# A graph and convolution layer on one core: the normalisation of the first batches on another engine, their turning and their rows issued as two streams, and both batch norms' constants asked for together

## The chip, the core and the metric

The kernel runs on one core of a Trainium2 chip. The metric is the device time of one execution in microseconds (us); the time before is the median of three runs, 2063.89 us (2061.74 to 2067.14). The engines are named as the profile names them: PE (TensorE, matrix products and turning), PEld (its weight loads), DVE (VectorE), ACT (ScalarE), POOL (GpSimd) and SP (SyncE, which issues most of the loads).

## The reference, cut to what matters

There are 32 batches of 512 nodes with 256 features. Each is normalised along its features and clipped at zero (h), and the layer's result is added to x:

```python
h = jnp.maximum(_layernorm(x, axis=-1), 0.0)
# inside the layer, on h:
c = relu(_bn(conv1(h), bn1))            # 1 tap
c = _bn(conv2(c), bn2)                  # 17 taps along the nodes
x_conv = relu(c + h)
s = h @ w_se.T + b_se                   # 3 values per node
A = exp(-|s_i - s_j|^2) * adj
x_nmp = A @ relu(h @ w_msg.T + b_msg)
gi, gh = [x_conv, x_nmp] @ w_ih.T + b_ih, h @ w_hh.T + b_hh
r, z = sigmoid(gi_r + gh_r), sigmoid(gi_z + gh_z)
out = x + (1 - z) * tanh(gi_n + r * gh_n) + z * h
```

The batch norm is an affine map per channel: scale = g / sqrt(v + eps), shift = b - m * scale. All data are 32-bit floats.

## The kernel before

Features lie on the partitions for all matrix work, so each batch is first normalised with its nodes on the partitions and then turned. The kernel is written as five streams (generators): *rows* (first convolution of each batch, written as rows into the tile h), *begins* (turning the batches from number 4 on), *graphs* (messages, kernel exponentials, masks, gather), *conv* (the second convolution, in a fast form of 25 products for each of seven groups of columns; the name ps_c) and *gates* (ps_acc). A planner in Python, which runs while the program is built, keeps an estimated time `now`, advanced by each TensorE instruction, and an estimated time at which DVE and ACT become free. It lets one stream issue at a time: the one that is furthest behind by its own clock among those whose condition holds. So the program is one fixed order on each engine, and each engine works its queue in that order. When no stream can issue, the planner waits in steps of 0.25 and now and then issues a transpose of the identity into an unused bank (`keep_warm`, line 143).

DVE and ACT work that no stream asks for directly comes from `fill` (line 1282): when DVE is free soon, `background` (line 1260) issues a piece of normalisation, of the second convolution's weights (`weights_first`, names g, gg, w, from the raw weights wraw) or of its operands (names x, xd).

The parts that the change and the steps of the prediction touch:

- `norm(b)` (line 349) normalises batch b in pieces. DVE makes the statistics of four chunks of 128 nodes (bn_stats, bn_aggr), adds eps (veps), POOL raises to the power -0.5 (`rsqrt`, line 275; names rstd), DVE makes the shift, and ACT applies scale and shift to each chunk, 128x256 (line 371). For batch 0 the chunks go in two halves.
- `begin(b)` (line 970) waits until batch b is normalised and calls `norm_t` (line 387) for each half of the features: four transposes on TensorE into a bank (ps_g), copied out with the clip at zero by ACT (hT). After the second half POOL stores hT to memory (hd). Batch 2 waits there until the messages of one graph have been issued (`told > 0`).
- `rows(g, b)` (line 1011) makes the first convolution of batch b: for each half of the outputs, products of w1 and hT into a bank, then three ACT operations into h with the first batch norm's scale and shift. `all_rows` (line 1306) does, for each of the four batches of the first group, first `begin(b)`, then a wait until ACT is free, then `rows(0, b)`.
- `graph(b)` (line 1020): messages (DVE adds the bias: msg, aug), `factors` (small DVE operations into aug, augl, augr), their transposes and copies (left, right), `kernel_exp` (line 906; four products of 5 rows, line 917, and four exponentials on ACT into at), `masked` (line 925: the mask m_sb is turned by TensorE and multiplied into at by DVE), `gather` (products of msg and at).
- `bn_affine(name)` (line 282) makes scale and shift of one batch norm: DVE adds eps, POOL takes the power, three DVE operations follow. It is called for bn1 and then for bn2 (line 1355), behind the normalisation of batch 0, and followed by three operations on the gates' biases (brz, bn) and then by the start of batches 1 to 3 (line 1369).

The four first batches have their x loaded ahead: batches 0 and 1 in x_sb, 2 and 3 in the tile y. Banks for turning, rows, messages, masks and gather come from one pool of three (ps_g).

## Time and profile before

| | us |
|---|---|
| median of the runs (lowest, highest) | 2063.89 (2061.74, 2067.14) |
| the profiled execution | 2063.59 |
| its span | 2061.8 |
| PE busy in the span | 2033.4 |
| DVE, ACT, POOL busy | 1319.6, 826.8, 451.7 |
| mean granted TensorE clock | 0.995 |

In the page, a group of instructions has a line such as "L127 DVE TENSOR_TENSOR msg<-ps_g,bmsg 128x256 ... x128 | 54.0, 422 | 192.2": line of the kernel, engine, operation, output and inputs, shape, count, busy us in total, mean ns of one, and idle time of the engine before it. Line 127 is the helper through which all DVE and ACT operations go, line 136 all matmuls, so the groups are told apart by their tiles. In the timeline a line gives the start, the time taken, the engine and the instruction, and in brackets how long the engine was idle before and who released it. TensorE carries each 32-bit matmul as two, so counts in the trace are twice those in the program.

### The profile page before, as it was taken

To read this page: it belongs to the slowest core of one execution; us is meant where nothing else is said; L and a number is where in the kernel's file an instruction comes from. 1 tells how busy PE (TensorE), PEld (TensorE's weight loads), DVE (VectorE), ACT (ScalarE), POOL (GpSimd) and SP (SyncE) were. 2 spreads that over 40 slices of the span, in tenths; PEclk is the share of its full clock that TensorE was granted. 3 is DMA by queue.
4 is the path that set the end of the run, shared out by engine and by line. 5 is a ranking of instruction groups with operands and counts; after the bars stand their busy time and mean duration, and the time that the engine had idled before them with its cause. 6 is when DMAs were issued, how large, how long until landed. Compare 5 with 4: busy or idle time off the path is not lost.

```text
span 2061.8 us, 25121 instructions
## 1 busy us (share of the span) xinstructions
PE 2033.4 (99%) x8621; PEld 1244.3 (60%) x8621; DVE 1319.6 (64%) x2378; ACT 826.8 (40%) x1585; POOL 451.7 (22%) x578
## 2 busy tenths in 40 slices
PE   8999999999999999999999999999999999999998
PEld 5878566666666656665566565566665666644444
DVE  6789677866777566765767664657766577532223
ACT  6544653343533446234453343533344423342221
POOL 2100122321312113221222221322211211133222
PEclk9999999999999999999999999999999999999999
DMA  7445778878988768896788876978866777555554
GB/s 288 154 174 189 250 219 222 196 207 204 228 226 204 186 182 241 195 215 176 190 218 195 209 184 152 231 187 198 198 178 176 190 168 159 149 113 97 62 92 36
DMA packets 539311, 378.29 MB, mean 183 GB/s; under 512 B 452992, under 2 KB 470432, under 8 KB 538048
## 3 DMA queue, kind: packets, MB, share of 16 engines
q1 hardware_dynamic: 381312, 278.74, 47.8%
q0 software_dynamic: 153184, 84.70, 23.8%
q10 hardware_dynamic: 4688, 13.24, 1.7%
q8 instruction: 69, 1.13, 0.2%
q14 instruction: 58, 0.48, 0.1%
HBM read 278.55 MB, written 114.56 MB: 191 GB/s over the span
## 4 chain that ended last, share of the span: by engine, by line
PE 60%; DVE 1%; issue 1%; DMA 1%; POOL 1%; ACT 0%; DVEq 0%; POOLq 0%; ACTq 0%
PE ps_acc L136 36%; PE ps_c L136 13%; PE ps_g L136 10%; DMA cd<-part 1%; PE ps_c L917 1%; PE ps_g L141 0%; POOL out_dram L1146 0%; POOL cd L721 0%; DVE o_sb L127 0%; DVE y L127 0%; DVE x L127 0%; DVE part L127 0%; ACT part L127 0%; DVE right L127 0%; PE ps_g L917 0%
## 5 line engine op out<-in xcount | busy, mean ns | idle before, releaser
L1146 POOL DMA_DIRECT2D out_dram<-o_sb x252 | 276.6, 1733 | 521.1 <-DVE o_sb L127 511.6
L136 PE MATMUL ps_acc<-xconv,wih 128*128 128x512 f32 (+1 forms) x772 | 361.5, 591 | 0.0
L136 PE MATMUL ps_acc<-xnb,wih 128*128 128x512 f32 (+1 forms) x772 | 359.0, 591 | 0.0
L136 PE MATMUL ps_acc<-hTb,whh 128*128 128x512 f32 (+1 forms) x772 | 356.1, 590 | 0.0
L136 PEld LDWEIGHTS ps_c<-xd,w 128*128 128x128 f32 x2304 | 288.5, 191 | 66.1 <-issue 56.1
L136 PEld LDWEIGHTS ps_c<-x,w 128*128 128x128 f32 x2032 | 256.0, 191 | 86.7 <-issue 65.4
L136 PE MATMUL ps_c<-xd,w 128*128 128x135 f32 (+1 forms) x2304 | 291.7, 280 | 1.7 <-ACT ps_c L127 1.4
L136 PE MATMUL ps_c<-x,w 128*128 128x135 f32 (+2 forms) x2032 | 265.6, 279 | 7.1 <-ACT n L127 2.6
L136 PE MATMUL ps_g<-at,msg 128*128 128x512 f32 x512 | 227.0, 593 | 1.6 <-DVE at L127 1.6
L136 PEld LDWEIGHTS ps_acc<-xconv,wih 128*128 128x128 f32 x772 | 140.7, 190 | 141.0 <-issue 139.2
L136 PEld LDWEIGHTS ps_acc<-xnb,wih 128*128 128x128 f32 x772 | 141.0, 190 | 140.1 <-issue 137.3
L136 PEld LDWEIGHTS ps_acc<-hTb,whh 128*128 128x128 f32 x772 | 140.7, 190 | 138.8 <-issue 136.7
L127 DVE TENSOR_TENSOR o_sb<-hTb,r 128x512 f32<-128x512 f32 x63 | 43.4, 689 | 212.6 <-ACT r L127 212.5
L127 DVE TENSOR_TENSOR msg<-ps_g,bmsg 128x256 f32<-128x256 f32 x128 | 54.0, 422 | 192.2 <-PE ps_g L136 192.0
L136 PEld LDWEIGHTS ps_g<-at,msg 128*128 128x128 f32 x512 | 95.2, 190 | 109.6 <-issue 103.9
L127 DVE SCALAR_TENSOR_TENSOR x<-x,x 128x544 f32<-128x544 f32 (+5 forms) x161 | 137.6, 854 | 2.7
L127 DVE TENSOR_TENSOR xd<-x 128x544 f32<-128x544 f32 (+1 forms) x144 | 102.5, 717 | 42.3 <-PE ps_c L136 42.2
L127 DVE TENSOR_TENSOR x<-x 128x272 f32<-128x272 f32 (+5 forms) x280 | 127.1, 498 | 0.3
L136 PE MATMUL ps_g<-wmsg,hTg 128*128 128x259 f32 x496 | 122.3, 382 | 0.0
L136 PE MATMUL ps_g<-hT,w 128*128 128x512 f32 (+8 forms) x296 | 119.3, 552 | 0.0
L127 ACT ACTIVATE ps_c<-ps_c 128x270 f32<-128x270 f32 (+1 forms) x144 | 56.6, 393 | 149.5 <-PE ps_c L136 149.4
L127 ACT ACTIVATE z<-ps_acc,brz 128x512 f32<-128x512 f32 x64 | 43.9, 686 | 179.0 <-PE ps_acc L136 179.0
(124 smaller groups left out, 2327.2 us busy)
## 6 DMA issues: line engine op xcount, KB each, us to landing
w<-wd SPq DMA_DIRECT2D x120, 768.0 KB, 5.7
m_sb<-in_adj_dram SPq DMA_DIRECT2D x384, 64.0 KB, 3.9
hT<-hd SPq DMA_DIRECT2D x33, 512.0 KB, 4.3
hd<-hT POOLq DMA_DIRECT2D x32, 512.0 KB, 6.0
hTb<-hd SPq DMA_DIRECT2D x32, 512.0 KB, 5.2
xnb<-nd SPq DMA_DIRECT2D x64, 256.0 KB, 2.9
out_dram<-o_sb POOLq DMA_DIRECT2D x252, 64.0 KB, 4.9
hTg<-hd SPq DMA_DIRECT2D x31, 512.0 KB, 4.3
```

Of the source, the lines that this page charges most:

```text
L127: getattr(self.engine, name)(*tiles, **more)
L136: nc.tensor.matmul(ps, lhsT, rhs, **more)
L917: nc.tensor.matmul(pss[c], gr.left[k, :], gr.right[k, :], start=True, stop=True, tile_position=(32 * c, 0),)
L1146: nc.gpsimd.dma_start(dst, src, accum_op=ALU.add)
```

## The change

Three things are edited. `norm(b)` applies scale and shift of batches 1, 2 and 3 by four DVE operations in one piece, where ACT did it in pieces of two chunks. Turning and rows of the four first batches become two streams, *firsts* and *rows*; batches 2 to 5 are now turned only when the rows of the batch two before have been issued. `bn_affine` asks for both powers first; the start of batches 1 to 3 and the statistics of batch 1 are issued before the scales and shifts are made of them.

```diff
+    def bn_affine():
+        names = ("bn1", "bn2")
...
+        for name in names:
+            rsqrt(rs[name], parts[name, "v"])
+        yield
+        for name in names:
...
+            yield sc, sh
...
             for c in range(c0, c0 + step):
+                if 0 < b < G:
+                    dve.tensor_scalar(
+                        xs[:, c, :], xs[:, c, :], rstd[:, c : c + 1], shift[:, c : c + 1],
+                        op0=ALU.mult, op1=ALU.add,
+                    )
+                    if c == NT - 1:
+                        yield dve.free + LAG
+                    continue
                 act.activation(
...
-        if b == 2:
-            yield lambda: told > 0
+        if b < G + 2:
+            yield lambda: b < 2 or told > 0 and rowed > b - 2
...
+    def all_firsts():
+        for b in range(G):
+            yield from begin(b)
+            first_at[b] = act.free + LAG
...
     def all_rows():
-        nonlocal rows_wait
+        nonlocal rows_wait, rowed
         for b in range(G):
-            yield from begin(b)
-            yield act.free + LAG
+            yield lambda: b in first_at
+            yield first_at[b]
             yield from rows(0, b)
+            rowed = b + 1
...
     streams = {
+        "firsts": (all_firsts(), 1e9, -3.0),
         "rows": (all_rows(), 1e9, -2.0),
...
-    bn1_sc, bn1_sh = bn_affine("bn1")
-    bn2_sc, bn2_sh = bn_affine("bn2")
+    NORM_AT[0] = act.free + LAG
+    affine = bn_affine()
+    next(affine)
+    load(1)
+    spare = cv.tile([P, 9 * NZ], F32, name="y")
+    for b in (2, 3):
+        at = (b - 2) * NT * D
+        load(b, spare[:, at : at + NT * D].rearrange("p (c d) -> p c d", d=D))
+    next(NORMS[1])
+    NORM_AT[1] = next(NORMS[1])
+    bn1_sc, bn1_sh = next(affine)
+    bn2_sc, bn2_sh = next(affine)
     brz = const.tile([P, 2 * ND], F32)
...
-    NORM_AT[0] = act.free + LAG
-    load(1)
-    spare = cv.tile([P, 9 * NZ], F32, name="y")
-    for b in (2, 3):
-        at = (b - 2) * NT * D
-        load(b, spare[:, at : at + NT * D].rearrange("p (c d) -> p c d", d=D))
```

More of the change, by code (lines that the diff above doesn't have):

```diff
@@ L280, in rsqrt @@
         nc.gpsimd.tensor_tensor(dst, t[:, :n], mhalf[:, :n], op=ALU.pow)
-    def bn_affine(name):
-        g, bb, m, v = (vec[:, _COL[f"{name}_{k}"] : _COL[f"{name}_{k}"] + ND] for k in "gbmv")
-        sc = const.tile([P, ND], F32, name=f"{name}_scale")
-        sh = const.tile([P, ND], F32, name=f"{name}_shift")
-        rs = front.tile([P, ND], F32, name="bn_rs")
-        rsqrt(rs, v)
-        dve.tensor_tensor(sc, g, rs, op=ALU.mult)
-        t = front.tile([P, ND], F32, name="bn_t")
-        dve.tensor_tensor(t, m, sc, op=ALU.mult)
-        dve.tensor_tensor(sh, bb, t, op=ALU.subtract)
-        return sc, sh
+    def bn_affine():
+        names = ("bn1", "bn2")
+        parts = {
+            (name, k): vec[:, _COL[f"{name}_{k}"] : _COL[f"{name}_{k}"] + ND]
+            for name in names for k in "gbmv"
+        }
+        rs = {name: front.tile([P, ND], F32, name=f"{name}_rs", bufs=1) for name in names}
+        for name in names:
+            rsqrt(rs[name], parts[name, "v"])
+        yield
+        for name in names:
+            sc = const.tile([P, ND], F32, name=f"{name}_scale")
+            sh = const.tile([P, ND], F32, name=f"{name}_shift")
+            dve.tensor_tensor(sc, parts[name, "g"], rs[name], op=ALU.mult)
+            t = front.tile([P, ND], F32, name="bn_t")
+            dve.tensor_tensor(t, parts[name, "m"], sc, op=ALU.mult)
+            dve.tensor_tensor(sh, parts[name, "b"], t, op=ALU.subtract)
+            yield sc, sh
     h1 = const.tile([P, Q * RV], F32)
@@ L1297, in all_graphs @@
             yield from graph(b)
+    first_at, rowed = {}, 0
+    def all_firsts():
+        for b in range(G):
+            yield from begin(b)
+            first_at[b] = act.free + LAG
     def all_begins():
```

## The prediction

> **What bounds the kernel now.** I read the page first, then the windows of the opening, then the timeline of its first 60 us, then the waits of TensorE up to 262 us.

> ```profile
> PE 2033.4 (99%) x8621; PEld 1244.3 (60%) x8621; DVE 1319.6 (64%) x2378; ACT 826.8 (40%) x1585; POOL 451.7 (22%) x578
> ...
> PE 60%; DVE 1%; issue 1%; DMA 1%; POOL 1%; ACT 0%; DVEq 0%; POOLq 0%; ACTq 0%
> ```

> The page: TensorE is busy 99% of the span and makes up nearly all of the chain that ended last. A change that removes no matrix work can only remove time in which TensorE waits or runs at a reduced clock. In the order in which the two built programs issue their instructions, each kind of TensorE work is there in the same number (2195 matmuls of the convolution, 1158 of the gates, and so on); only the warming transposes go from 39 to 42. By the 600th matmul of the convolution both programs have issued the same amount of everything else, and the last 1934 of some 4500 TensorE instructions are the same in the same order. So the effect is made in the first 260 us, and whatever TensorE gains or loses there is simply carried to the end.

> The windows of the opening (columns: stretch, its length, then busy us and count for PE, PEld, DVE, ACT, POOL, the granted clock, DMA share, GB/s):

> ```profile
> 18.29:21.70 3.41, 2.24 (x14) 1.74 (x15) 2.81 (x14) 3.41 (x8) 0.20 (x1) 1.00 1.02 425
> 21.70:25.11 3.41, 3.41 (x13) 1.69 (x13) 2.54 (x3) 2.38 (x7) 1.39 (x2) 1.00 0.99 400
> 25.11:28.52 3.41, 3.08 (x12) 1.40 (x11) 3.38 (x3) 3.41 (x9) 0.27 (x1) 1.00 1.05 395
> 28.52:31.94 3.42, 3.42 (x8) 1.39 (x6) 1.11 (x1) 1.49 (x3) 0.26 (x1) 0.50 1.08 387
> 31.94:35.36 3.42, 3.42 (x5) 1.35 (x5) 0.00 (x0) 1.70 (x5) 0.00 (x0) 0.50 0.32 131
> ```

> ScalarE is full from 18.3 to 21.7 and from 25.1 to 28.5 (3.41 of 3.41). From 28.52 to 35.36 TensorE runs at half clock and VectorE does nothing. The cuts at every 3.41 us are my choice: the clock changes at 8.05, 11.46, 28.52 and 35.36, which are 1, 5 and 2 such steps apart. The timeline shows who holds whom:

> ```profile
> 17.28 1.08 ACT L127 ACTIVATE x_sb<-x_sb,shift,rstd 128x256 f32<-128x256 f32 x2
> ...
> 21.11 3.60 PE L136 MATMUL ps_g<-hT,w 128*128 128x512 f32 x8
> ...
> 25.89 1.08 ACT L127 ACTIVATE y<-y,shift,rstd 128x256 f32<-128x256 f32 x2
> ...
> 26.88 1.07 ACT L127 ACTIVATE hT<-ps_g 128x512 f32<-128x512 f32 x2
> ...
> 30.00 6.26 PE L136 MATMUL ps_g<-hT,w 128*128 128x512 f32 x8
> ...
> 36.81 0.69 DVE L127 TENSOR_TENSOR at<-ps_g,at 128x512 f32<-128x512 f32 x1 [7.18 <-PE ps_g L141]
> ...
> 38.48 3.60 PE L136 MATMUL ps_g<-hT,w 128*128 128x512 f32 x8
> ```

> The rows of batch 1 (21.11), 2 (30.00) and 3 (38.48) wait for ScalarE, which normalises, copies the turned tiles out (hT) and makes the exponentials in one queue. Behind the rows of batch 2, at half clock 6.26 us instead of 3.60, VectorE sits idle 7.18 us until the first mask is turned.

> **The change part by part.** (1) Both batch-norm powers are asked for together. Before, VectorE waits 0.81 and 0.80 us for them and starts the statistics of batch 1 at 10.38. After, it starts them at about 7.4 (that x has landed by then is taken from its landing times: asked for by about 1.8, median 5.0). Four chunks and veps take 2.25 us as before, so GpSimd's rstd of batch 1 ends near 11.0 instead of 13.9. The nine small constant operations follow at 9.8 to 11.2; their first user is ScalarE's h at 12.57, so they cost nothing; if the cover went, it would be their own 1.4 us.

> (2) Twelve ScalarE normalisations go: two take 1.09 us, so 6.5 us. VectorE gains twelve TENSOR_SCALAR of 128x256, a form that the trace lacks. The rows around it:

> ```profile
> L127 DVE TENSOR_SCALAR augl<-aug 128x12 f32<-128x12 f32 x32 | 5.5, 172 | 0.0
> L127 DVE TENSOR_SCALAR z<-z 128x512 f32<-128x512 f32 x1 | 0.4, 427 | 0.0
> L127 DVE TENSOR_TENSOR msg<-ps_g,bmsg 128x256 f32<-128x256 f32 x128 | 54.0, 422 | 192.2 <-PE ps_g L136 192.0
> ```

> Between 172 ns for 12 elements and 427 for 512, 256 lie at 0.30 us: 12 x 0.30 = 3.6 us, the value I take, since it is the same operation. The high end is the two-input row, 12 x 0.42 = 5.0 us; the low end 12 x 0.17 = 2.1. [...] The two rows above put the fixed part alone at 0.166 us.

> (3) The chain, with these durations in the new order. Batch 1: shift at 13.6, but its four normalisations stand behind the first message addition (15.16), so they end at 16.9 instead of 18.4; the later message additions slip 1.2 us, and the banks that turning needs come free at 17.5 and 18.0. ScalarE does hT from 18.1 to 19.2 (before 19.77 to 20.8), the copy of augr ends at 19.3, and the rows of batch 1 start at 20.0, **1.1 us earlier**. Batch 2: normalised by 21.7 on VectorE, turned at 23.5 behind these rows; ScalarE's queue no longer has y (1.08 us) ahead of hT, so hT runs from 24.95 instead of 26.88, the last exponent product from 26.1 instead of 27.5, and the rows of batch 2 start at 27.4, **2.6 earlier**. Batch 3: normalised by 25.4; the four wraw operations (7.0 us, first at 22.62 before) run 25.4 to 32.4 instead of ending at 29.6, inside the idle 7.18 us.

> (4) The clock. If TensorE keeps full clock, the rows of batch 2 end at 30.9; then turning of batch 3, h (31.1 to 32.4), hT (to 33.5), and the rows of batch 3 start at S = 33.6. If the clock halves at 28.52 for one step, 1.7 us are lost and S = 35.3. Before, S = 38.48. I take full clock: the step from 18.29 to 21.70 held only 0.6 us of rows and stayed full, and the step from 25.11 to 28.52, which before held no full matmul, would now hold 1.1 us of rows. Against it: from 23.5 to 27.4 TensorE has nothing but transposes and exponent products for 3.9 us; before, it was 24.5 to 30.0, and the clock fell in it. [...]

> (5) What eats part of it. Before, TensorE goes from the rows of batch 3 to two masks, the gather (43.90, S + 5.4) and the messages, which end at 54.4 = S + 15.9. In the new order masks 1 to 3 stand behind these rows, and VectorE has x<-h (1.68 us, after h at S + 4.95), then mask 2, two x and one combination (1.9), then mask 3: done at S + 9.9. The gather starts at S + 10 and the messages end at S + 20.5. Of that wait 1.85 us carry half of the first product, so equal work is done at S + 18.6: 52.2 at full clock, 53.9 at half. Against 54.4 that is **-2.2 or -0.5 us**.

> (6) From there to 262. TensorE's waits before sum to 10.1 us, the largest 2.1 (ps_c on ACT w, at 102.3 to 104.4, with five warming transposes among the masks of batch 2), and at 253 to 260 the clock of 0.70 and 0.50 costs another 3.1 us. In the new order the masks of batch 2 have one warming transpose and those of batch 3 seven: that stall moves, it does not go. I put this stretch at 0, with -6 (both gone) and +4 (a second stall with its clock step) as ends. Queues: the loads on SP keep their order up to the reading back of batch 2's hd, and GpSimd's store of hT 0 stands behind one rstd as before, now at about 11.1 instead of 13.85; no store is read back before 29.16.

> Sum, against the profiled execution's 2063.59 us (span 2061.8 and 1.8 around it; 0.3 under the median of the runs): -2.2 + 0 = **2061.4 us**.

> **Rivals.** *The clock takes it:* the rows of batch 2 fall to half clock; -0.5 here and about +1 from shifted waits: 2064. For it: the 3.9 us gap; against: 1.1 us of rows in that step. *The stalls go with it:* VectorE comes out of the opening ahead (the statistics of batch 4 are done before the messages of batch 1), so the wait at 102 (2.8 us with the gaps between its masks) and the clock loss at 253 (3.1) vanish: 2063.6 - 2.2 - 5.9 = 2055.5. For it: both are by-products of which engine is late; against: the warming transposes only moved. *VectorE takes over:* it is busy 9.5 to 10 of 10 us at 60 to 80, 90 to 110 and 130 to 150; if the twelve operations cost the 5.0 us of the high end, and the new places between the masks leave it no idle to hide them in, all 5.0 go to the end, with one half-clock step (1.7): 2070.3, slower. It decides once the first mask operation of batch 0 is no earlier than 36.8. Against: the idle 7.18 us. That the change doesn't do what it says is excluded by the order: the twelve operations stand on VectorE, and the powers together.

> **Numbers.** Forecast 0.45 (own range 2058.5 to 2064), clock 0.18, stalls gone 0.22, VectorE 0.15. About 0.3% (6 us) is what a measurement of this kernel can tell from no change. Faster by more: the third case and a tail of the first, 0.25. Slower by more: most of the fourth, 0.13. Within: 0.62. The range runs from the third case with the twelve operations at their low end (2055.5 - 1.5 = 2054.0) to the fourth, 2070.3.

> **What would show it.** Statistics of batch 1 at about 7.4; TENSOR_SCALAR x_sb and y at 0.30 us; rows of batches 1 to 3 at 20.0, 27.4 and 33.6; clock 1.00 from 28.5 to 35.4; the first mask operation at about 33; the gather at 43.6; wraw done at 32.4. I am wrong if rows start early and the gather of batch 0 is later than 45, if x is not there at 7.4, or if the next batches give back or add more than 4 us.

## The result, and the profile after

The changed kernel takes 2076.88 us (median of six runs, 2074.13 to 2080.01); the kernel before, run beside it, 2064.76 (2061.74 to 2067.65). The ratio is 1.0056, 95% interval 1.0045 to 1.0067: **about 12 us slower**. The forecast was 2061.4, and the time lies outside its range (2054.0 to 2070.3). The profiled execution took 2077.6 us, its span is 2075.8, that is 14.0 more than the 2061.8 of the execution profiled before.

The page after, busy us of each engine, and the shares of the chain that ended last:

```profile
span 2075.8 us, 25101 instructions
...
PE 2039.6 (98%) x8624; PEld 1248.6 (60%) x8624; DVE 1324.6 (64%) x2390; ACT 822.9 (40%) x1573; POOL 454.5 (22%) x578
...
PE 93%; DVE 3%; ACT 2%; DMA 1%; issue 0%; SPq 0%; ACTq 0%; DVEq 0%
```

TensorE is busy 6.2 us longer with the same products and three more warming transposes (2039.6 against 2033.4), and idle for 36.2 us of the span (2075.8 - 2039.6) where it was 28.4: 6.2 slower and 7.8 idle make the 14.0. VectorE and ScalarE now have 3% and 2% of the chain that ended last (before, 1% and 0%).

The opening, in the same stretches of 3.41 us as before (columns as there):

```profile
18.29:21.70 3.41, 3.10 (x20) 2.31 (x19) 3.27 (x18) 2.89 (x6) 0.60 (x1) 1.00 1.03 433
21.70:25.11 3.41, 3.41 (x15) 1.78 (x13) 2.07 (x9) 2.00 (x5) 1.04 (x1) 1.00 0.99 401
25.11:28.52 3.41, 3.41 (x11) 1.77 (x11) 3.35 (x6) 3.41 (x8) 0.59 (x1) 0.84 1.06 399
28.52:31.94 3.42, 3.42 (x6) 1.31 (x6) 3.38 (x3) 0.61 (x3) 0.00 (x0) 0.66 1.06 384
31.94:35.36 3.42, 2.93 (x17) 1.93 (x16) 1.62 (x2) 2.97 (x8) 0.00 (x0) 1.00 0.33 132
```

ScalarE is no longer full from 18.3 to 21.7 (2.89 of 3.41), TensorE is, and VectorE works through the stretch from 28.5 to 31.9 in which it was idle for two thirds (3.38 in place of 1.11). The slow clock covers one stretch of about 3 us instead of two. The timeline of the same time:

```profile
16.66 1.37 DVE L127 TENSOR_SCALAR x_sb<-x_sb,rstd,shift 128x256 f32<-128x256 f32 x4
...
20.73 3.60 PE L136 MATMUL ps_g<-hT,w 128*128 128x512 f32 x8
21.08 1.35 DVE L127 TENSOR_SCALAR y<-y,rstd,shift 128x256 f32<-128x256 f32 x4
...
25.14 1.38 DVE L127 TENSOR_SCALAR y<-y,rstd,shift 128x256 f32<-128x256 f32 x4
...
28.19 4.92 PE L136 MATMUL ps_g<-hT,w 128*128 128x512 f32 x8
...
35.24 0.69 DVE L127 TENSOR_TENSOR at<-ps_g,at 128x512 f32<-128x512 f32 x1 [1.80 <-PE ps_acc L146]
```

The rows of batches 1 and 2 start at 20.73 and 28.19 (before 21.11 and 30.00), those of batch 3 at 35.08 (38.48), and VectorE's idle time ahead of the first mask is 1.80 instead of 7.18 us. So the opening did what it was to do. The loss is made later. TensorE's waits over the whole run (us in total, times, longest):

```profile
PE ps_c L136 <- ACT z L127: 4.4, 3, 2.2
PE ps_c L932 <- ACT n L127: 3.7, 2, 2.4
PE ps_c L136 <- ACT at L127: 3.2, 1, 3.2
PE ps_c L136 <- DVE x L127: 3.2, 2, 2.1
PE ps_g L136 <- DVE at L127: 2.2, 1, 2.2
```

Before, the longest of TensorE's waits was 2.1 us and no group of them summed to more than 2.6. One of the two for x stands in the opening, at 42.76; the others stand at 147, 183, 257, 267, 308, 714 and 762 us (and a small one at 232), where the change edits nothing.

**Where the 14 us are.** TensorE issues its products in a fixed order that the planner writes. In the following table they are numbered as the program issues them (the trace carries a matmul as two records, a transpose as one: before, 2316 records for the 1158 products of the gates, 128 for the 32 masks of four transposes each), without the warming transposes and the small exponent products (the numbers of 183, 187, 702 and 963 further down count the latter too), and kernels are compared only at numbers up to which both kernels have issued exactly the same products. It gives the time at which the product ends in the kernel before, and how much later (+) or earlier each other kernel is there; e1, e4 and e5 are experiments below that keep the order of before, e2 and e3 have that of the changed kernel:

```
products   before |    e1     e4     e5 |  after     e2     e3
      49    36.26 | -1.97  -3.60  -1.07 |  -3.15  -3.75  -4.11
     101    56.31 | -1.97  -1.31  -1.08 |  -0.86  -1.42  -0.58
     452   147.34 | -1.96  -1.60  -1.07 |  -1.38  -0.36  +0.42
     600   195.55 | -1.96  -1.60  -1.08 |  +3.39  +1.23  +3.70
     757   259.91 | -1.96  -1.58  -1.06 |  +3.29  +0.61  +3.70
    1030   372.53 | -1.95  -1.55  -1.39 | +12.43 +11.45 +12.84
    1216   456.84 | -1.95  -1.54  -1.38 | +13.68 +12.69 +14.08
    1343   522.98 | -1.96  -1.55  -1.40 |  +8.95  +9.34 +10.08
    1684   674.80 | -1.86  -1.65  -1.45 |  +9.69 +10.06 +10.79
    1869   765.15 | -1.80  -1.68  -1.50 | +15.04 +15.42 +16.14
    2600  1108.91 | -2.69  -2.20  -1.53 | +13.99 +14.73 +13.40
```

The changed kernel is 0.9 us ahead at 56 us and 1.4 at 147. It loses 4.8 us from 147 to 196, 9.1 from 260 to 373 and 5.4 from 675 to 765, and gains 4.7 from 457 to 523. From about 1042 us on, where the orders join for good, the difference stays at 13.99 to the end.

The largest of these stretches begins so. TensorE of the changed kernel, then of the kernel before at the same work:

```profile
266.93 1.20 PE L136 MATMUL ps_c<-x,w 128*128 128x136 f32 x8 [2.16 <-ACT z L127]
267.97 0.60 PE L141 MATMUL ps_g<-ident,m_sb 128*128 128x128 f32 x4
270.08 2.13 PE L136 MATMUL ps_c<-xd,w 128*128 128x136 f32 x16 [1.51 <-ACT ps_c L127]
```

```profile
260.86 0.60 PE L141 MATMUL ps_g<-ident,m_sb 128*128 128x128 f32 x4
261.30 1.88 PE L136 MATMUL ps_acc<-xconv,wih 128*128 128x512 f32 x4
263.01 1.88 PE L136 MATMUL ps_acc<-xnb,wih 128*128 128x512 f32 x4
264.73 1.10 PE L136 MATMUL ps_c<-x,w 128*128 128x136 f32 x8
265.67 0.60 PE L141 MATMUL ps_g<-ident,m_sb 128*128 128x128 f32 x4
266.10 1.88 PE L136 MATMUL ps_acc<-hTb,whh 128*128 128x512 f32 x4
267.82 2.02 PE L136 MATMUL ps_c<-xd,w 128*128 128x136 f32 x16
```

The first part of a product of the second convolution (ps_c<-x) waits until ScalarE has read the product ahead out of its bank, and the next part (ps_c<-xd) until ScalarE has copied the first (ps_c<-ps_c). Before, products of the gates (ps_acc) stand between them, 3.4 and 1.7 us of work that waits for nothing new, and TensorE has no gap. In the new order only a turned mask stands there, and TensorE waits 2.16 and 1.51 us. The work is the same; what fills the time is elsewhere.

Behind some of the waits TensorE also runs slow. Windows of TensorE in the changed kernel (stretch, length, busy, granted clock, DMA share, GB/s):

```profile
147.17:150.50 3.33, 3.33 (x16) 0.53 0.95 315
183.50:185.00 1.50, 1.50 (x3) 0.82 1.07 291
185.00:188.00 3.00, 3.00 (x5) 0.52 0.78 164
266.00:270.00 4.00, 1.64 (x12) 1.00 0.73 234
307.50:309.40 1.90, 1.89 (x8) 0.50 0.00 0
765.80:768.60 2.80, 2.80 (x5) 0.58 0.14 22
```

Behind the waits at 147, 183, 308 and 762 the clock is at half for 3.41 us each (it falls at 146.91, 184.45, 307.33 and 764.72); behind that at 267 it is not. Two more such stretches begin at 259.55 and 983.17. In the kernel before, the only such place after 50 us, until the last few us of the span, is at 253.81 to 260.64, two stretches long. So the changed kernel has six stretches of 3.41 us at half clock where the kernel before has two; half of TensorE's busy time in them is 9.9 against 3.0 us, which is about the 6.2 us by which its products are slower.

### The profile page after: what moved, and what is told of

It reads as the page before. It is cut to its first block, busy times and chain, and to the rows that moved or that the text cites. A ratio compares the mean times of both kernels' runs of the same rounds, so it can differ in the third digit from the quotient of the medians.

```text
span 2075.8 us, 25101 instructions
## 1 busy us (share of the span) xinstructions
PE 2039.6 (98%) x8624; PEld 1248.6 (60%) x8624; DVE 1324.6 (64%) x2390; ACT 822.9 (40%) x1573; POOL 454.5 (22%) x578
## 4 chain that ended last, share of the span: by engine, by line
PE 93%; DVE 3%; ACT 2%; DMA 1%; issue 0%; SPq 0%; ACTq 0%; DVEq 0%
PE ps_acc L136 47%; PE ps_c L136 23%; PE ps_g L136 20%; PE ps_g L141 1%; PE ps_c L932 1%; DVE x L127 1%; ACT y L127 0%; DVE y L127 0%; DVE at L127 0%; DVE z L127 0%; DMA m_sb<-in_adj_dram 0%; PE ps_acc L932 0%; ACT x_sb L127 0%; DVE g L127 0%; DVE gg L127 0%
## 5 line engine op out<-in xcount | busy, mean ns | idle before, releaser
L136 PE MATMUL ps_acc<-xconv,wih 128*128 128x512 f32 (+1 forms) x772 | 362.6, 592 | 0.0
L136 PE MATMUL ps_acc<-xnb,wih 128*128 128x512 f32 (+1 forms) x772 | 360.2, 592 | 0.0
L136 PE MATMUL ps_acc<-hTb,whh 128*128 128x512 f32 (+1 forms) x772 | 355.8, 591 | 0.0
L136 PEld LDWEIGHTS ps_c<-xd,w 128*128 128x128 f32 x2304 | 288.3, 191 | 65.7 <-issue 57.4
L136 PEld LDWEIGHTS ps_c<-x,w 128*128 128x128 f32 x2032 | 258.3, 193 | 90.6 <-issue 62.8
L136 PE MATMUL ps_c<-xd,w 128*128 128x135 f32 (+1 forms) x2304 | 290.8, 279 | 1.8 <-ACT ps_c L127 1.8
L136 PE MATMUL ps_c<-x,w 128*128 128x135 f32 (+2 forms) x2032 | 268.1, 281 | 13.4 <-ACT z L127 4.1
L136 PE MATMUL ps_g<-at,msg 128*128 128x512 f32 x512 | 228.8, 597 | 3.2 <-DVE at L127 2.2
L136 PEld LDWEIGHTS ps_acc<-hTb,whh 128*128 128x128 f32 x772 | 141.3, 190 | 144.3 <-issue 142.1
L136 PEld LDWEIGHTS ps_acc<-xconv,wih 128*128 128x128 f32 x772 | 141.6, 191 | 143.0 <-issue 140.4
L136 PEld LDWEIGHTS ps_acc<-xnb,wih 128*128 128x128 f32 x772 | 141.4, 191 | 138.9 <-issue 136.2
L127 DVE TENSOR_TENSOR msg<-ps_g,bmsg 128x256 f32<-128x256 f32 x128 | 53.9, 422 | 213.2 <-PE ps_g L136 213.1
L127 DVE TENSOR_TENSOR o_sb<-hTb,r 128x512 f32<-128x512 f32 x63 | 43.4, 689 | 195.2 <-ACT r L127 195.1
L136 PEld LDWEIGHTS ps_g<-at,msg 128*128 128x128 f32 x512 | 95.5, 191 | 112.6 <-issue 105.8
L127 DVE TENSOR_TENSOR xd<-x 128x544 f32<-128x544 f32 (+1 forms) x144 | 102.8, 717 | 59.6 <-PE ps_c L136 59.0
L127 DVE SCALAR_TENSOR_TENSOR x<-x,x 128x544 f32<-128x544 f32 (+5 forms) x161 | 137.5, 854 | 2.9
L127 DVE TENSOR_TENSOR x<-x 128x272 f32<-128x272 f32 (+5 forms) x280 | 126.6, 496 | 0.3
L136 PE MATMUL ps_g<-wmsg,hTg 128*128 128x259 f32 x496 | 122.6, 382 | 0.9 <-DVE aug L127 0.9
L127 ACT ACTIVATE ps_c<-ps_c 128x270 f32<-128x270 f32 (+1 forms) x144 | 56.8, 394 | 166.4 <-PE ps_c L136 166.3
L136 PE MATMUL ps_g<-hT,w 128*128 128x512 f32 (+8 forms) x296 | 119.0, 551 | 0.1
L127 ACT ACTIVATE z<-ps_acc,brz 128x512 f32<-128x512 f32 x64 | 44.0, 687 | 188.0 <-PE ps_acc L136 188.0
```

Source lines behind the costliest of these rows:

```text
L127: getattr(self.engine, name)(*tiles, **more)
L136: nc.tensor.matmul(ps, lhsT, rhs, **more)
```

## The experiments

T1: the change is harmless, and what costs is that the planner, fed with other bookings, writes another order for TensorE behind the opening. R1: VectorE's added work, or the masks' wait on it, costs. R2: one part of the change costs by itself. The planner writes the queues of all engines, so with TensorE's order those of VectorE, ScalarE and the loads change too (VectorE's queue in e2 has only its first 48 and last 940 of 2378 instructions as in the kernel before); no run here tells them apart, and "the order" below stands for all of them. All kernels below compute the whole of the reference. In the order that they ran, with the planner's own time (`now`) when its last stream ends, which needs no chip:

| kernel | TensorE's order | planner's end | median, us | ratio to before (95%) | span | TensorE idle in it |
|---|---|---|---|---|---|---|
| before | old | 2045.50 | 2064.76 | 1 | 2061.8 | 28.4 |
| after | new | 2052.25 | 2076.88 | 1.0056 (1.0045, 1.0067) | 2075.8 | 36.2 |
| e1 | old | 2045.50 | 2064.17 | 0.9990 (0.9979, 1.0001) | 2059.1 | 27.1 |
| e2 | new | 2052.50 | 2075.91 | 1.0049 (1.0035, 1.0062) | 2076.5 | 38.7 |
| e3 | new | 2052.50 | 2076.72 | 1.0047 (1.0033, 1.0061) | 2075.2 | 37.2 |
| e4 | old from 183 | 2046.50 | 2062.27 | 0.9983 (0.9973, 0.9994) | 2059.8 | 27.4 |
| e5 | old | 2045.25 | 2064.01 | 0.9995 (0.9987, 1.0003) | 2060.3 | 27.4 |
| e6 | old from 187 | 2045.75 | 2067.42 | 1.0015 (1.0006, 1.0024) | 2063.8 | 28.8 |
| e7 | a third | 2051.75 | 2073.86 | 1.0040 (1.0027, 1.0053) | 2072.2 | 33.7 |
| e8 | new to 702, then another | 2048.00 | 2074.25 | 1.0039 (1.0026, 1.0053) | 2074.6 | 33.1 |
| e9 | old | 2045.25 | 2064.41 | 0.9993 (0.9985, 1.0002) | 2058.8 | 27.5 |
| e10 | as e4 | 2046.50 | 2060.94 | 0.9977 (0.9968, 0.9985) | 2059.2 | 24.3 |
| e11 | as e4 to 963, then another | 2052.50 | 2065.41 | 1.0002 (0.9993, 1.0011) | 2064.8 | 31.4 |

Each ratio is against runs of the kernel before on the same chip (medians there 2066.07 for e1 to e4, 2064.78 for e5 to e8, 2065.25 for e9 to e11).

**e1: the work moved, the order kept.**

```diff
             for c in range(c0, c0 + step):
+                if 0 < b < G:
+                    nc.vector.tensor_scalar(
+                        xs[:, c, :], xs[:, c, :], rstd[:, c : c + 1], shift[:, c : c + 1],
+                        op0=ALU.mult, op1=ALU.add,
+                    )
+                    act.free = max(act.free, now) + act.fixed + act.each * D
...
+                    continue
                 act.activation(
```

> The kernel before, with batches 1 to 3 normed by VectorE, but booked by the planner as ScalarE's, so that TensorE's order of products is the one of the kernel before to the last instruction. Theory T1 (the loss is a different written order after the opening, not the work that was moved): 2064 us, within 3 us of the kernel before (2064.8). Theory R1 (VectorE's 4 us of added work, or the masks' wait on it, is what costs): 2069 to 2077.

Measured 2064.17, ratio 0.9990. At equal work it is 1.96 us ahead from the 49th product to the 1343rd without a change (table above). VectorE's twelve operations cost nothing at the end: R1 falls, for the old order; e2 shows the same in the new one.

**e2: the order changed, the work kept.**

```diff
+                if 0 < b < G:
+                    nc.scalar.activation(
+                        xs[:, c, :], xs[:, c, :], AF.Identity,
+                        bias=shift[:, c : c + 1], scale=rstd[:, c : c + 1],
+                    )
+                    dve.free = max(dve.free, now) + dve.fixed + dve.each * D
...
+                    continue
                 act.activation(
```

> The kernel before, norming left on ScalarE, but booked by the planner as VectorE's, so that TensorE's order is the changed kernel's to the last instruction; no work is moved between engines. T1: 2074 to 2079 (the changed kernel: 2076.9). R1: 2062 to 2067, because VectorE has nothing more to do. The cost of a wrong booking itself (ScalarE later than the books say in the opening) should be under 2 us.

Measured 2075.91, ratio 1.0049. Nothing but the planner's bookkeeping differs from the kernel before, and the whole loss is there, at the same products, and with the same waits (4.9, 3.7, 3.2, 3.2 and 2.2 us in the five groups shown for the changed kernel). The written order is the cause.

**e3: the norming alone, booked as what it is.**

```diff
+                if 0 < b < G:
+                    dve.tensor_scalar(
+                        xs[:, c, :], xs[:, c, :], rstd[:, c : c + 1], shift[:, c : c + 1],
+                        op0=ALU.mult, op1=ALU.add,
+                    )
+                    if c == NT - 1:
+                        yield dve.free + LAG
+                    continue
```

> The kernel before with VectorE's norming alone, booked as such: TensorE's order is the changed kernel's, without the edit of the batch norms' constants and without the two streams. T1: 2075 to 2079. R1: 2069 to 2077. R2 (the constants asked for together, or the two streams, are the cause): 2062 to 2067.

Measured 2076.72, ratio 1.0047, without streams and without the edit of the constants. R2 falls for those two.

**e4: the whole change, the old order.** To the changed kernel:

```diff
                 at_product = m + 1
+                if at_product == 1:
+                    now += -1
```

> The whole change, with the planner's time put back once by 1.0 us after the first product, which gives TensorE the order of the kernel before from its 183rd product on to the end. T1: 2061 to 2065, the 1 to 2 us that the opening gains and no more. R1 and R2: 2074 to 2078, as the changed kernel, since all of its work and its opening is there.

Measured 2062.27, ratio 0.9983: 14.6 us under the changed kernel, by one number in the planner, with all of the change's work. It is faster than both kernels; its gain at equal work, 1.6 to 2.2 us, is that of the opening and is carried to the end.

**e5: the constants alone.** Of the change, only `bn_affine` and the earlier start of batch 1:

```diff
+    affine = bn_affine()
+    next(affine)
+    load(1)
...
+    next(NORMS[1])
+    NORM_AT[1] = next(NORMS[1])
```

> The kernel before with the edit of the batch norms' constants alone (norming on ScalarE, one stream for the rows). TensorE's order is that of the kernel before to the last instruction. T1 (only the order costs): 2062 to 2066, within 3 us of the kernel before, a gain of at most the 3 us by which the sums of batch 1 start earlier. R2 (one part of the change costs by itself, here the constants): 2069 to 2077.

Measured 2064.01, ratio 0.9995: 1.07 us ahead at equal work in the opening, 1.53 at product 2600; in the medians that is within what the interval leaves open.

**e6: norming and streams, without the constants.** The norming as in e3, and

```diff
     streams = {
+        "firsts": (all_firsts(), 1e9, -3.0),
```

> VectorE's norming and the two streams, without the edit of the constants. The planner happens to come back to the order of the kernel before: the same from its 187th product on, and the planner's own time at its end is 2045.75 (before: 2045.50; the changed kernel: 2052.25). T1: 2061 to 2066. R2, if the streams with the norming are what costs: 2074 to 2078.

Measured 2067.42, ratio 1.0015: 1.4 us over the range, though far from R2's. At equal work it is 3.2 us ahead at product 49 and 1.7 behind at 101 (56 us). TensorE waits 3.43 us for VectorE's masks ahead of the gather of batch 0, which starts at 43.96 (before 43.90), so the lead is gone, and the gather itself takes 8.80 us instead of 7.13, with a granted clock of 0.54 from 46 to 49. From product 210 to 1869 it stays within 0.4 us behind, then falls back by 0.8 at 797 us, where a wait for ScalarE is 1.47 instead of 0.62, and by 1.7 behind 959 us, where the gates' products take 3.14 us instead of 1.88 in the same order. So the old order again keeps the loss of 12 us away; what is left is the masks' wait, that the prediction had in its step 5, this wait for ScalarE and TensorE's clock.

**e7: the streams alone.** As e6 without the norming.

> The two streams alone, norming on ScalarE, constants as before. TensorE gets a third order, which joins the other two only after 2281 of its 4467 products; the planner's own time at its end is 2051.75, 6.25 over that of the kernel before. T1: 2068 to 2078, the chip confirming the planner's own loss at about once to twice its size. If the streams' work and not the order counted, the time would be that of the norming with streams in the old order, 2061 to 2066.

Measured 2073.86, ratio 1.0040. A third order, again a loss: +9.5 at product 646, +14.1 at 845, +10.3 from 2500 on. The work is that of the kernel before.

**e8: the new order to 229 us, then another.** To the changed kernel:

```diff
                 at_product = m + 1
+                if at_product == 24:
+                    clock["graphs"] += 0.15
```

> The changed kernel with one number moved: the planner's clock of the stream of graphs put forward by 0.15 after product 24. TensorE has the changed kernel's order up to its 702nd product (about 229 us), and another one behind it; the planner's own time at its end is 2048.0 in place of 2052.25. T1, with the loss made in three stretches (147 to 196 us: 4.8; 260 to 373: 9.4; 675 to 765: 6, less 4.6 given back at 457 to 523): the first of them stays and the others go or change, 2066 to 2071. R1 or R2 (work or opening): 2075 to 2078, since nothing of them is changed.

A miss: 2074.25, ratio 1.0039. The stretch from 260 to 373 did lose its price (product 1377, at 540 us: 5.6 us **ahead** of the kernel before), but the new order has other places further on: 1.3 behind at product 2173 (906 us), 4.5 at 2961 (1300 us), 12.8 at 4081 (1839 us), with waits of 2.31, 1.09 and 2.17 at 780, 1237 and 1419. The timeline of the last:

```profile
1419.14 2.17 PE L136 MATMUL ps_c<-x,w 128*128 128x135 f32 x8 [2.17 <-ACT at L127]
1421.10 3.62 PE L136 MATMUL ps_acc<-hTb,whh 128*128 128x512 f32 x4
```

The two take 1.08 and 1.88 us elsewhere in this kernel: the wait of 2.17 has 2.8 us of half clock behind it. So the loss is not one bad place that could be mended; a new order has new places. The run also shows luck: its first 702 products are those of the changed kernel, with the same waits, but its rows of batch 2 took 3.60 instead of 4.92, the products at 146 us took 2.04 instead of 3.53 and the gather behind the wait of 2.16 took 7.13 instead of 8.83. It is 0.64 ahead of before at product 600 where the changed kernel was 3.39 behind.

**e9: norming and constants, without streams.** e1 and e5 in one kernel.

> VectorE's norming (booked as ScalarE's) and the constants asked for together, without the two streams; TensorE's order is that of the kernel before to the last instruction. T1: what the norming alone (1.96 us at equal work) and the constants alone (1.1 us) gave in their own runs, together at most 3 us: 2061 to 2064. If something in the two parts together costs, 2065 or more.

Measured 2064.41, ratio 0.9993, 0.4 us over the range. 4.62 us ahead at product 101, 2.96 at 452, 2.94 at 2600: more than e1 and e5 in the opening, part of it lost before 147 us, and too little in the medians to tell from e1.

**e10: the whole change in the old order, warmed by real products.** To e4:

```diff
         for _ in range(n):
-            nc.tensor.transpose(unused[:, :P], ident, ident)
+            nc.tensor.matmul(unused[:, :P], ident, ident, start=True, stop=True)
```

> The whole change in the old order (as in e4: 2062.3), but the 34 or so products that only keep TensorE warm are real products of 128x128 in place of transposes. Theory C1 (only real products count for TensorE's clock): the rows of batch 0 at 9.5 run at full clock, 3.6 us in place of 5.4, those of batch 2 at 27.7 in 3.6 in place of 4.9, less up to 3 us that the warming itself takes longer: 2059 to 2062. Theory C2 (a stretch goes slow by its place in fixed windows of time, whatever the warming is): 2062 to 2065, with the rows still at 4.9 to 5.6 us.

Measured 2060.94, ratio 0.9977, the lowest of all, though its interval overlaps that of e4. All 41 warming products are real ones here, the 18 that open the kernel too. The rows of the four first batches:

```profile
9.62 3.70 PE L136 MATMUL ps_g<-hT,w 128*128 128x512 f32 x8
18.72 3.60 PE L136 MATMUL ps_g<-hT,w 128*128 128x512 f32 x8
26.03 3.60 PE L136 MATMUL ps_g<-hT,w 128*128 128x512 f32 x8
31.70 3.60 PE L136 MATMUL ps_g<-hT,w 128*128 128x512 f32 x8
```

All at full speed. With transposes for warming, the rows of batch 0 took 3.98 to 5.63 us in the profiles of twelve kernels, those of batch 2 from 3.60 (e2, e7, e8, e9, e11) to 6.26 (before). So the rows of batch 2 say nothing for C1, and those of batch 0 little: where 3.98 can come by luck, 3.70 may as well. Against C1 as it is put there is a step of the clock in e8 that held 2.13 us of transposes and no product, and the clock stayed full behind it (last section). e10 is 2.9 us ahead of e4 at product 100 and 2.7 at 1900, and gives 2.2 of that back by 963 us (1.7 of them from 956 to 959, at half clock), so that 0.6 is left.

**e11: one number after product 30.** To e4:

```diff
+                if at_product == 30:
+                    clock['graphs'] += -0.08
```

> The whole change in the old order (as in e4: 2062.3) with one number moved: the planner's clock of the stream of graphs put back by 0.08 after product 30. TensorE's order is that of e4 for its first 963 products (about 342 us) and another one behind them; the planner's own time at its end goes from 2046.5 to 2052.5. T1: 2069 to 2076, the loss made by order alone, in places that no part of the change touches, and each wait of TensorE with half clock behind it. R1 and R2: 2060 to 2065, as e4.

The two orders part behind 326 us of e4's profile (the 963rd product), not 342. A miss in size: 2065.41, ratio 1.0002, some 4 us over e4 (0.9983) where 7 to 14 were expected. At equal work the profiled execution is 2.70 ahead of e4 to product 900 (its opening, the same instructions, ran at a better clock: the rows of batch 0 took 3.98 us, those of e4 5.40) and 5.02 behind from 4055 on: the order cost 7.7 us in this profile, about the planner's 6.0. The largest single place:

```profile
960.14 2.17 PE L136 MATMUL ps_c<-x,w 128*128 128x135 f32 x8 [2.96 <-ACT z L127]
962.11 5.70 PE L136 MATMUL ps_g<-at,msg 128*128 128x512 f32 x8
```

A wait of 2.96, and 3.2 us more in the two groups behind it than they take elsewhere (1.08 and 3.60).

## Why the prediction was wrong, step by step

1. *The constants.* The statistics of batch 1 start at 7.87 (said: 7.4; before 10.38); veps waited for the vectors' load until 7.72. The nine small operations cost nothing, as said, and the statistics of batch 1 are half a microsecond late. Right in the main; e5 measures the part alone at 1.1 to 1.5 us.
2. *The twelve operations.* Said 0.30 us each, 3.6 in all; measured 1.37 + 1.35 + 1.38 = 4.1 us, 0.34 each from start to start (0.40 as the mean duration, in which the rows of the prediction are given), inside the bounds of 0.17 and 0.42.
3. *The chain.* Rows of batch 1 at 20.73 (said 20.0), of batch 2 at 28.19 (27.4), wraw done at 33.4 (32.4). The common 0.7 to 1.0 us come from the rows of batch 0, which took 5.63 us instead of the 4.41 of before, so that everything behind them started later. Right but for that. (VectorE does not do nothing from 28.52 on in the kernel before, as the prediction has it: it works until 29.6, 1.11 us of the first 3.42, and only then stands idle.)
4. *The clock.* I took full clock; it fell to 0.50 from 27.44 to 30.85, and the rows of batch 3 started at 35.08, where 35.3 stood for half clock. The places of the steps, 25.11 and 28.52, were taken over from the profile before; in the changed kernel's they are 24.02 and 27.44, and the step between holds none of the 1.1 us of rows that were counted on. In e8's profile the same instructions ran the rows of batch 2 in 3.60. So neither case was the right one to take alone. That transposes keep the clock up less than products do is not shown: e10, with real products in their place, would fit that with 3.70 for the rows of batch 0; but in e8 TensorE has nothing but transposes from 141.90 to 145.32 (2.13 us), and the clock stays full behind them. Transposes alone do not explain the falls. In the kernel before, 2.68 of the 3.08 busy us from 25.11 to 28.52, ahead of the fall, are products of five rows.
5. *What eats part of it.* Said at equal work after the messages: -2.2 at full clock or -0.5 at half. Measured -0.86 in the changed kernel, -3.34 in e8, -1.31 in e4 (product 101). The gather started at 44.82, 9.7 us behind the rows of batch 3 (said: 10). The size of the gain was right, and e4 carries it to the end (-2.0 in the span).
6. *From there to 262, and the rest.* Here it failed. From product 101 to 757 the changed kernel loses 4.2 us, where 0 was put and -6 and +4 were given as ends: at the far one, and just past it. And the first part says: "So the effect is made in the first 260 us, and whatever TensorE gains or loses there is simply carried to the end." **This is the step that was wrong.** It rests on two counts, equal amounts by the 600th product of the convolution and the same last 1934 products. The second is right. The first is right but for two products of the gates; yet the 600th product stands at 413 us of the profile before, not at 260, and equal amounts are not an equal order: between the 50th product and about 1042 us the orders differ again and again, and 10.7 of the 14.0 us are made after 260 us. What the prediction put at nothing, the 800 us behind its opening, is where TensorE waits more and runs slower. In e1, where the order is indeed the same, the carrying holds: 1.97 us ahead at product 49 and 1.96 at 1343, 2.69 at 2600.

Of the rivals, *the stalls go with it* named the right kind of thing, stalls as by-products of the order, with the wrong sign and end point. *VectorE takes over* had the right sign and the wrong cause: e1 has the same operations on VectorE and is not slower. No rival was "another order for the next 800 us", though the planner's own end time, 2045.50 against 2052.25, was there to be read. It gives the sign here and not the size: 6.75 for the 14.0 measured.

Why any new order tends to lose: TensorE is busy 99% of the span and waits only 15 us in all from 50 to 1100 us before, so there was little to win behind the opening. This is an argument; four orders are few. Of the four orders with a planner's end of 2048 or more (new, e7, e8, e11), three are slower by 0.39 to 0.56%, and the fourth is level with a kernel that it would have beaten by 0.2% in the old order. What stays open: how much of the 6.2 us of slower products would go if TensorE were kept busy in all of these waits. That was not tried; the kernel issues no warming behind 214 us, and the gates, from whose banks (ps_acc) the warming's is taken, begin at 249 us.

## What to carry to other kernels

Where a planner writes the instruction order, an edit has two effects: on the work, and, through the bookings, on the order of everything behind it; separate them by keeping the order while moving the work, and the other way round (e1 and e2), before blaming an engine. Read the planner's own end time first: the kernels in which it was 2046.5 or less came out at 0.9977 to 1.0015 of the time before, those with 2048 or more at 1.0002 to 1.0056. It does not rank the latter: e8 with 2048.00 lost 0.39%, e11 with 2052.50 only 0.02%. Counting equal amounts of work is no proof of equal order; compare the two lists of instructions place by place, and compare times only at points of equal work.
